# Splitting weights into halves beside attention: loads two parts ahead, stores half a step later, spread over 1.3 batches instead of 0.97

## The chip, the cores and the metric

The kernel runs on one core of one Trainium2 chip. The core has a matrix engine (TensorE, PE in the profile; its weight loads are PEld), VectorE (DVE), ScalarE (ACT), GpSimd (POOL), and SyncE (SP), which here issues every DMA. The engines run side by side, each through its own instructions in a fixed order, and wait for each other and for DMAs by semaphores. The metric is the device time of one execution in microseconds (us).

## The reference, cut to what matters

Eight sequences of 64 rows by 512 pass through six sublayers, each added to its input: cross attention with 32 heads on 8 key/value heads over a context of 1601 rows, a state space layer, a ternary feed forward layer, a second cross attention without weights, causal self attention, and an octonion feed forward layer. The change touches only the preparation of some weights, among them the output projection `Wo` of the first sublayer:

```python
q = (query @ Wq + bq).reshape(B, L, NKV, G, HDIM)
k_, v_ = jnp.split(kv @ Wkv + bkv, 2, axis=-1)
...
attn = jax.nn.softmax(scores, axis=-1)
o = jnp.einsum('bkglm,bmkd->blkgd', attn, v).reshape(B, L, NHEAD * HDIM)
return o @ Wo + bo
```

## The kernel before

**Halves.** Most products are computed in a format that carries fewer bits than float32. To keep the precision, an operand is split into a rounded part (high) and the rest (low), and a product is the sum of high x high, high x low and low x high, three matmuls. `split` (L100) does it with two instructions: ACT rounds a copy (L105, or L65 where the order is pinned), and DVE or POOL subtracts (L106). Weights that are used again and again are split once and stored in DRAM as pairs of halves.

**The main line.** `x_all` (L517) walks through 8 batches of 8 key/value heads, 64 units of about 41 us. A unit consists of six steps. In them stand the keys of the unit (`x_k`, L354: 12 matmuls of k_ps for each of four blocks of the context; the first block of the next unit is made in the last step), the values (`x_v`, v_ps, L334), the scores (`x_s`, s_ps, L385), and, for the unit before, the maximum (`x_max` L403, `x_spread` L412), the exponentials (`x_exp`: DVE adds at L426, ACT exponentials at L427, POOL sums at L429, L446, L448 and L452), their product with the values (`x_av`, o_ps, L464) and the end (`x_o`). In step 3 the key weights wk of the next unit are loaded (`x_w`, L346), in step 4 its queries q (L351). There is one buffer for wk, so its load can start when the last k_ps of the unit that reads it is done, and the next unit's first k_ps needs it some 8 us later. During batch 0 the queries of the next unit are computed as well (`q_head`, L252) and stored (d_q, L283); that unit's q is loaded from there.

After each unit of an odd batch `x_wo` (L492) applies the output projection to that unit's heads of two batches: four tiles of `Wo` halves are loaded (L508, wo<-d_wo, 512 KB each) and used in three matmuls each (w_ps, L511). `x_wo(1, 0)`, the first, adds the input and the bias bo before (L500, L501). It runs during unit (1, 2).

**Beside it.** Generators are advanced between the main line's pieces: `advance` (L1314) compares the cost that the main line has yielded, in units of a batch (`X_COST` = 236), with a generator's start, end and total cost, and runs its next pieces. `halves` (L606) is one of them: from 0.1 to 0.97 batches it loads, splits and stores 56 parts of 128 x 512: 32 of `Wo`, 8 of `W_outT`, 16 of `attnT` (queues L614, L617; d_wo, d_wout, d_wat). `prep` (L620) runs from the first unit of batch 1 to 2.0 batches and prepares the feed forward weights. After two batches the other five sublayers of those two follow as generators, too; the last pair's forms the tail, after the main line.

**Buffers.** The parts of `halves`, bo and the tiles of `x_wo` share one tag, "wo", with `WOB` = 3 buffers. A tile that finds no free buffer waits until an earlier one is released: a part, when its store has landed; a tile of `x_wo`, when its matmuls are done.

**The order of the work.** The program is recorded in Python order, and a scheduler then orders each engine's instructions by its own estimate of when they can start, with the program's order as priority. `Side` (L68) pins a generator's instructions on DVE, ACT and POOL to the program's order; DMAs on SP are not pinned. On the chip each engine goes through the resulting order, and an instruction that waits holds all behind it.

Of the kernel before, what the change touches and what calls it, by code (L numbers as in the profile page):

```python
# [8 lines left out]
FP = mybir.dt.float32  # L9
FR = mybir.dt.float32r  # L10
# [6 lines left out]
P = 128  # L17
D = 512
# [19 lines left out]
WOB = 3  # L38
# [40 lines left out]
class Kernel:  # L79
# [526 lines left out]
    def halves(self):  # L606

        nc, i = self.nc, self.i
        todo = [(i["Wo"][k * G + g], self.wo_s[k][:, g]) for k in range(NKV) for g in range(G)]
        todo += [(i["W_outT"][h], self.wout_s[h]) for h in range(NCH)]  # L610
        todo += [(i["attnT"][m, c], self.wat_s[m][c]) for m in range(4) for c in range(NC)]
        for src, dst in todo:
            t = self.sb("wo", [P, 2, D], FR, pool=self.xp, bufs=WOB)
            nc.sync.dma_start(out=t[:, 1].bitcast(FP), in_=src)  # L614
            yield 0.5
            self.split(t[:, 0], t[:, 1], t[:, 1].bitcast(FP), eng=nc.gpsimd)
            nc.sync.dma_start(out=dst, in_=t.bitcast(FP))  # L617
            yield 0.5

    def prep(self):  # L620
# [664 lines left out]
    def run(self):  # L1285
# [22 lines left out]
        def start(gen, now, cost, end):  # L1308
            env = {k: getattr(self, k) for k in ENV}
            if not self.tail:  # L1310
                env["nc"] = Side(self, PINNED)
            side.append({"gen": gen, "cost": cost, "got": 0.0, "t0": now, "end": end, "env": env})
# [18 lines left out]
        gi, now, xdone = 0, 0.0, 0.0  # L1331
        start(self.halves(), HALVES_START, HALVES_COST, HALVES_END)
        for cost, fin in self.x_all(list(range(B))):
# [33 lines left out]
SPAN = [3.1,3.1,2.6,0.2]  # L1367
PREP_END = 2.0
HALVES_START = 0.1
HALVES_END = 0.97  # L1370
HALVES_COST = 56.0
MAMBA_TAGS = ("a2", "lv", "bc", "xpad", "sm")
FFN_TAIL = (("l", 0), ("l", 1), ("a", 0), ("l", 2), ("a", 1), ("d", 0), ("a", 2), ("d", 1), ("d", 2))
# [116 lines left out]
```

## Time and profile before

| | |
|---|---|
| three runs | 2689.3 us median (2683.2 to 2691.5) |
| profiled execution | 2687.2 us, its span 2685.1 us |
| mean granted clock of PE | 0.983 |
| PE busy | 2549.7 us, 95% of the span |
| ACT, POOL busy | 1350.2 us (50%), 1247.6 us (46%) |
| casts of halves (ACT, L65, tile wo) | 56 of 0.62 us, from 86.3 to 379.4 us |
| subtractions of halves (POOL, L65, tile wo) | 56 of 1.29 us |
| `x_wo`'s matmuls (L511) | 384, from 420.2 to 2384.4 us |
| ACT's waits for loads of parts, 86 to 382 us | 26.8 + 11.2 + 5.8 us |
| DMA, median from issue to landing | wo<-d_wo 5.3 us, d_wo<-wo 5.7, d_wat<-wo 4.7, wo<-in_attnT 4.4; wk from 90 to 380 us 4.6 |

A line of waits reads: the engine and its line, what released it, the microseconds in total, how often, and the longest. A line of the timeline reads: start, duration, engine and line, operation, output<-input, count, and in brackets the idle time before and what ended it; SPq is SP's queue of DMA issues, and an issue's duration is that of the issue, not of the transfer. A line of windows reads: from:to, length, busy time (instructions), granted clock (1.00 is full speed), mean busy share of the 16 DMA engines, GB/s.

### The profile page before, as it was taken

To read this page: it belongs to the slowest core of one execution; us is meant where nothing else is said; L and a number is where in the kernel's file an instruction comes from. 1 tells how busy PE (TensorE), PEld (TensorE's weight loads), DVE (VectorE), ACT (ScalarE), POOL (GpSimd) and SP (SyncE) were. 2 spreads that over 40 slices of the span, in tenths; PEclk is the share of its full clock that TensorE was granted. 3 is DMA by queue.
4 is the path that set the end of the run, shared out by engine and by line. 5 is a ranking of instruction groups with operands and counts; after the bars stand their busy time and mean duration, and the time that the engine had idled before them with its cause. 6 is when DMAs were issued, how large, how long until landed. Compare 5 with 4: busy or idle time off the path is not lost.

```text
span 2685.1 us, 43976 instructions
## 1 busy us (share of the span) xinstructions
PE 2549.7 (95%) x16320; PEld 2269.3 (85%) x16320; DVE 1667.6 (62%) x2739; ACT 1350.2 (50%) x3128; POOL 1247.6 (46%) x1243
## 2 busy tenths in 40 slices
PE   7999999999999999999999999999999999977797
PEld 6988999999999899978989988988898898964544
DVE  4534357665687775545567676554657777668754
ACT  4545454344556554544555554544546545436433
POOL 2434463463368663521367457521239556405420
PEclk9999999999999999999999999999999999987899
DMA  9788876675213244764324452665343455466674
GB/s 308 225 295 276 281 239 190 203 240 180 67 66 105 68 133 150 232 190 145 97 98 148 149 161 89 216 201 164 102 135 92 137 159 155 143 226 216 234 261 166
DMA packets 311126, 466.08 MB, mean 174 GB/s; under 512 B 88440, under 2 KB 187768, under 8 KB 306432
## 3 DMA queue, kind: packets, MB, share of 16 engines
q1 hardware_dynamic: 310912, 463.28, 53.4%
q8 instruction: 128, 2.10, 0.3%
q14 instruction: 86, 0.70, 0.1%
HBM read 389.66 MB, written 73.53 MB: 173 GB/s over the span
## 4 chain that ended last, share of the span: by engine, by line
PE 68%; DMA 9%; DVE 9%; POOL 7%; issue 4%; ACT 3%; SPq 0%; POOLq 0%; DVEq 0%; ACTq 0%
PE v_ps L334 16%; PE k_ps L363 16%; PE o_ps L464 10%; PE s_ps L385 8%; POOL a L65 3%; PE w_ps L511 2%; PE acc L274 2%; DVE a L65 2%; PE acc L1077 2%; PE acc L801 2%; PE acc L1021 1%; PE acc L759 1%; PE acc L756 1%; POOL ss L452 1%; DMA b<-in_ctxT_dram 1%
## 5 line engine op out<-in xcount | busy, mean ns | idle before, releaser
L363 PE MATMUL k_ps<-cxb,wk 128*128 128x384 f32 x2304 | 470.3, 347 | 35.3 <-DVE mx L392 13.2
L334 PE MATMUL v_ps<-wv,cxb 128*128 128x256 f32 x3456 | 467.9, 281 | 1.0 <-DVE kt L109 0.6
L334 PEld LDWEIGHTS v_ps<-wv,cxb 128*128 128x128 f32 x3456 | 438.0, 188 | 19.3 <-issue 11.7
L363 PEld LDWEIGHTS k_ps<-cxb,wk 128*128 128x128 f32 x2304 | 405.3, 191 | 53.2 <-DVE mx L392 15.6
L464 PE MATMUL o_ps<-S,v 128*128 128x256 f32 (+1 forms) x1664 | 413.6, 381 | 7.4 <-DVE rw L479 4.0
L385 PE MATMUL s_ps<-q,kt 128*128 128x256 f32 (+1 forms) x2496 | 413.7, 299 | 5.2 <-DVE mx L392 2.4
L385 PEld LDWEIGHTS s_ps<-q,kt 128*128 128x128 f32 (+1 forms) x2496 | 342.8, 185 | 28.5 <-issue 6.9
L388 ACT COPY S<-s_ps 128x512 f32<-128x512 f32 (+1 forms) x448 | 241.9, 553 | 241.0 <-PE s_ps L385 236.6
L452 POOL TENSOR_TENSOR ss<-ss,S 128x512 f32<-128x512 f32 x254 | 349.3, 1375 | 14.7 <-ACT S L427 1.3
L392 DVE TENSOR_TENSOR mx<-s_ps,mx 128x512 f32<-128x512 f32 x256 | 175.1, 684 | 264.0 <-ACT S L388 262.7
L464 PEld LDWEIGHTS o_ps<-S,v 128*128 128x128 f32 (+1 forms) x1664 | 298.6, 190 | 46.7 <-issue 5.2
L429 POOL TENSOR_TENSOR ss<-S,S 128x512 f32<-128x512 f32 x64 | 84.5, 1320 | 469.4 <-ACT S L427 469.1
L108 ACT ACTIVATE kt<-k_ps,c_bk 128x384 fp32r<-128x384 f32 (+1 forms) x256 | 152.0, 594 | 246.9 <-PE k_ps L363 245.9
L426 DVE TENSOR_TENSOR S<-S,m_ps 128x512 f32<-128x512 f32 (+1 forms) x448 | 257.3, 640 | 20.5 <-PE m_ps L412 20.2
L427 ACT ACTIVATE S<-S 128x512 f32<-128x512 f32 (+1 forms) x448 | 246.7, 599 | 43.4 <-DVE S L426 42.7
L109 DVE SCALAR_TENSOR_TENSOR kt<-k_ps,c_bk,kt 128x384 fp32r<-128x384 f32 (+1 forms) x256 | 160.9, 629 | 158.0 <-ACT kt L108 156.5
L337 ACT COPY v<-v_ps 128x256 f32<-128x256 f32 (+1 forms) x416 | 152.5, 368 | 198.4 <-PE v_ps L334 196.0
L334 PE MATMUL v_ps<-wv,cxt 128*128 128x256 f32 (+1 forms) x1536 | 206.5, 282 | 1.5 <-DVE mx L392 1.0
L334 PEld LDWEIGHTS v_ps<-wv,cxt 128*128 128x128 f32 (+1 forms) x1536 | 192.7, 175 | 10.5 <-issue 3.4
L65 DVE TENSOR_TENSOR_SCAN a<-a,a 128x512 f32<-128x512 f32 x96 | 154.7, 1613 | 62.9 <-POOL a L65 62.8
L363 PE MATMUL k_ps<-cxt,wk 128*128 128x450 f32 x768 | 178.6, 375 | 1.4 <-DVE mx L392 1.3
L65 POOL TENSOR_TENSOR a<-a,bc 128x512 f32<-128x512 f32 x96 | 128.1, 1335 | 90.7 <-DVE a L65 90.7
(357 smaller groups left out, 3947.8 us busy)
## 6 DMA issues: line engine op xcount, KB each, us to landing
wo<-d_wo SPq DMA_DIRECT2D x128, 512.0 KB, 5.3
wk<-d_wk SPq DMA_DIRECT2D x63, 512.0 KB, 3.5
wv<-d_wv SPq DMA_DIRECT2D x31, 1024.0 KB, 5.7
cst<-in_ctxT_dram SPq DMA_DIRECT2D x96, 192.0 KB, 3.0
b<-in_ctxN_dram SPq DMA_DIRECT2D x36, 512.0 KB, 3.7
d_q<-q_t SPq DMA_DIRECT2D x32, 512.0 KB, 5.9
q<-d_q SPq DMA_DIRECT2D x64, 256.0 KB, 3.1
d_wo<-wo SPq DMA_DIRECT2D x32, 512.0 KB, 5.7
```

Of the source, the lines that this page charges most:

```text
L65: return lambda *a, **k: self.tc.keep_in_program_order(f(*a, **k))
L109: eng.scalar_tensor_tensor(lo, src, bias, hi.bitcast(FP), ALU.add, ALU.subtract)
L334: nc.tensor.matmul(ps[:r], lhsT=cx[:, a, c, o : o + r], rhs=w[:, m, c, :], start=k == 0, stop=k == 11)
L337: nc.scalar.copy(vt[:r], ps[:r])
L363: nc.tensor.matmul(ps[:, :wd], lhsT=w[:, a, c, :], rhs=cx[:, m, c, :], start=k == 0, stop=k == 11)
L385: nc.tensor.matmul(sp[:r, gi, :], lhsT=kt[:, a, o : o + r], rhs=q[:, m, :], start=k == 0, stop=k == 2)
L388: nc.scalar.copy(s[:r, :n], sp[:r, :n])
L392: nc.vector.tensor_tensor(mx, sp, S[0] if len(S) == 1 else mx, ALU.max)
L426: nc.vector.tensor_tensor(sv, sv, ps[:r, 1:2].to_broadcast([r, w, 256]), ALU.add)
L427: nc.scalar.activation(sv, sv, AF.Exp, scale=ISC)
L452: nc.gpsimd.tensor_tensor(ss, ss, S[n], ALU.add)
L464: nc.tensor.matmul(ps[:, 0], lhsT=self.v[(b, j, t)][:r, hc : hc + P], rhs=S[t // 2][:r, t % 2], start=t == 0, stop=t == NT - 1)
```

## The change

`halves` keeps its parts, their order and the instructions for each. Before, a step was: take a buffer and load; half a step later split and store. Now two loads are issued at the start; a step is: split; half a step later store, and load the part after the next one. The total cost is the same, and the end goes from 0.97 to 1.3 batches. `WOB` remains 3.

```diff
-        for src, dst in todo:
-            t = self.sb("wo", [P, 2, D], FR, pool=self.xp, bufs=WOB)
-            nc.sync.dma_start(out=t[:, 1].bitcast(FP), in_=src)
+        ts = {}
+
+        def load(k):
+            if k < len(todo):
+                ts[k] = self.sb("wo", [P, 2, D], FR, pool=self.xp, bufs=WOB)
+                nc.sync.dma_start(out=ts[k][:, 1].bitcast(FP), in_=todo[k][0])
+
+        load(0)
+        load(1)
+        yield 1
+        for k, (src, dst) in enumerate(todo):
+            t = ts.pop(k)
+            self.split(t[:, 0], t[:, 1], t[:, 1].bitcast(FP), eng=nc.gpsimd)
             yield 0.5
-            self.split(t[:, 0], t[:, 1], t[:, 1].bitcast(FP), eng=nc.gpsimd)
             nc.sync.dma_start(out=dst, in_=t.bitcast(FP))
+            load(k + 2)
             yield 0.5
...
-HALVES_END = 0.97
+HALVES_END = 1.3
```

## The prediction

> **What bounds the kernel now.** I read the page's first three parts, then the waits of TensorE (PE) and of SP's queue, then time windows.
>
> ```profile
> span 2685.1 us, 43976 instructions
> PE 2549.7 (95%) x16320; PEld 2269.3 (85%) x16320; DVE 1667.6 (62%) x2739; ACT 1350.2 (50%) x3128; POOL 1247.6 (46%) x1243
> ```
>
> PE is busy 95% of the span, so whatever delays PE counts in full, and waits of ScalarE (ACT) and GpSimd (POOL) count only where PE ends up waiting for them. PE's waits from 20 to 335 us, where the halves run:
>
> ```profile
> PE k_ps L363 <- DMA wk<-d_wk: 9.2, 5, 4.1
> PE acc L274 <- DVE q_t L109: 1.3, 1, 1.3
> ```
>
> Five times PE stands before the next head's keys, until the tile wk has landed. SP's own waits from 90 to 380 us say what held wk's load back:
>
> ```profile
> SPq L614 <- DMA d_wo<-wo: 68.4, 27, 6.5
> SPq L617 <- POOL wo L65: 32.0, 25, 3.7
> SPq L614 <- DMA d_wat<-wo: 20.0, 9, 5.8
> SPq L614 <- DMA d_wout<-wo: 18.6, 8, 4.7
> SPq L351 <- DMA d_q<-q_t: 10.5, 6, 3.2
> ```
>
> SP issues in order. 139 us of these 290 it stands before loads of halves (L614, 107 us, until an earlier store has left one of the three `wo` buffers) or before their stores (L617, 32 us, until POOL is done); wk's load stands behind. The worst case, SP and then PE:
>
> ```profile
> 180.25 1.72 SPq L247 DMA_DIRECT2D q_w<-in_Wq_dram  x1
> 182.06 1.28 SPq L617 DMA_DIRECT2D d_wo<-wo  x1
> 185.23 0.33 SPq L351 DMA_DIRECT2D q<-d_q  x1
> 185.61 0.46 SPq L346 DMA_DIRECT2D wk<-d_wk  x1
> ...
> 191.35 3.84 PE L363 MATMUL k_ps<-cxb,wk 128*128 128x384 f32 x12 [4.09 <-DMA wk<-d_wk]
> ```
>
> The buffer of wk was free at 179.59 (end of the last matmul that reads it); its load is issued 6.0 us late. PE by windows (time, busy, granted clock):
>
> ```profile
> 170.00:210.00 40.00, 35.91 (x213) 0.96 0.82 265
> 210.00:250.00 40.00, 38.01 (x235) 1.00 0.87 294
> 330.00:380.00 50.00, 47.18 (x314) 1.00 0.83 278
> 380.00:420.00 40.00, 40.00 (x276) 1.00 0.57 190
> 420.00:460.00 40.00, 40.00 (x274) 1.00 0.52 154
> ```
>
> From 90 to 380 us PE idles 12.0 us (9.2 for wk, 2.8 around the batch's end, 335 to 370 us), and one clock dip costs 40 x 0.04 = 1.6 us. So **13.6 us is all that the change can win** there. From 380 us, when the halves are done, PE idles nothing.
>
> **The change, part by part.** No arithmetic and no byte is added: 56 loads, 56 casts (622 ns), 56 subtractions (1292 ns), 56 stores, as before.
>
> *Loads two ahead.* SP is not pinned to program order, and the loads already go as soon as a buffer is free:
>
> ```profile
> 6.62 1.97 SPq L614 DMA_DIRECT2D wo<-in_Wo_dram  x3
> ```
>
> Three are issued by 8.6 us, the first cast runs at 86.3. The built program keeps the pattern: each load follows the store that frees its buffer. This edit alone I cost at nothing. *Stores half a step later*: the scheduler again places them by readiness, directly ahead of q and wk in five heads of seven, as before: nothing. [...]
>
> *Spread to 1.3 batches.* Before, 56 parts take 86 to 379 us, 5.2 us each, for 0.87 batches. Over 1.20 batches that is 404 us, 7.2 each, to about 490. If a part holds SP as long as now, SP is held 139/404 = 34% of the time and not 48%: x 0.72. The lateness of the six wk loads that count (from the end of the last matmul on the old wk to the issue at L346) is 0.8, 4.0, 6.0, 6.9, 3.5, 3.3 us, 24.5 in all. Of it 10.5 is q's load waiting for d_q to land, which the change does not touch; the other 14.0 shrinks to 10.1. So lateness falls by 16%, 3.8 us over the last five, which are the ones that PE waited for; each falls by less than PE's wait, so all 3.8 of the 9.2 us are saved. Of the 2.8 at the batch's end I take 1.2, of the clock's 1.6 half: **gain 5.8 us**, between 0 and 13.6.
>
> *What the longer spread runs into.* From `x_wo(1, 0)` on (PE 420 us), the output projection takes the same three `wo` buffers. Before, the halves had left them:
>
> ```profile
> 381.45 0.33 SPq L617 DMA_DIRECT2D d_wat<-wo  x1
> 381.83 1.26 SPq L508 DMA_DIRECT2D wo<-d_wo  x2
> ```
>
> The weights of `x_wo` were called 38 us ahead, and PE never waited long for them. After, some ten parts are still to come. The order in which the built program stands on SP, with what each waits for:
>
> ```
> store part A (POOL); store part B (POOL)
> load bo      (A's store landed: its buffer)
> load w0      (B's store landed)
> load w1      (POOL's add of bo)
> load part C  (PE has used w0)
> load w2      (PE has used w1)
> store part D (POOL); load wk
> load w3      (D's store landed)
> ```
>
> On PE, after the spread of the maximum (L412), stand 13 o_ps matmuls in a row, each waiting for an exponential, then w_ps with w0, and v_ps, s_ps and k_ps behind; before, that work stood between them. In the clock of the old trace: part B is cast after the copy of v at 419.68 (0.37), so at 420.05 + 0.62; POOL 1.29 gives 422.0; a d_wat store lands in 4.7 (426.7), w0 in 5.3: 432.0. PE is through the spread at 420.6 (mc is ready at 420.12). The adds (L426, 0.64 us each) and exponentials (L427) let the 13th o_ps go at 426, with 13 x 0.216 = 2.8 us of work in it. PE idles 432.0 - 420.6 - 2.8 = **8.6 us**. With the shortest landing seen for these tiles (2.6) and for w (4.3) it is 5.5; with the longest (8.0 and 7.4) 14.0.
>
> Three smaller ones. w3, behind D's store: 0.9 us. Casts of two parts whose loads wait until PE has used w3 stand on ACT before the next head's kt: 0.2 + 4.4 (load) + 0.62 + 0.59 + 0.63 = 6.4 us against 5.25 us of matmuls ahead (0.7 + 2.1 + 1.4 + 1.05): 1.2. The head after that repeats the pattern with fewer o_ps (nine) and one part ahead of w0: about 2.9, estimated at a third of the first. Together 5.0, between 0 and 7. The stall of six us before w0 is longer than the 4.09 us gap that was followed by the clock of 0.96, so I add its 1.6. **Loss 8.6 + 5.0 + 1.6 = 15.2 us**, between 5.5 and 22.6. [...]
>
> *Elsewhere.* The built program's order on PE is the old one again from the last heads of batch 1 to the tail; in the tail the scheduler orders anew. Nothing removed or added; PE idles 68 of the last 385 us, so a new order can win or lose: 0, with 5 us to both sides.
>
> **Sum.** 15.2 - 5.8 = +9.4 us on the profiled execution's 2687.2 (span 2685.1 and 2.1 around it), that is 2696.6. The median of the three runs is another 2.1 us higher, 2689.3; on it the sum gives 2698.7. I forecast **2698**.
>
> **Rivals.** *The gain comes whole, the projection's weights are in time* (faster). If wk is never late, 13.6 us come back; if the w loads reach the queue before the parts do, since the real stores land in 2.6 us or POOL is ahead, what is left of the loss is about 3. 2689.3 - 13.6 + 3 = 2679. It decides where w0 lands before PE's 13th o_ps, 6 us sooner than I reckon. For it: SP's 139 us are large, PE's gaps are all here. Against: w0 needs two landings in sequence after B's cast. *A wash.* The same waits, spread wider: gain 5, loss at its low end 5.5: 2690. For it: after 420 us SP and POOL are less loaded (DMA share 0.52 against 0.85), so landings are short. *Worse.* All three heads that overlap stall like the first, or the tail's new order costs 5 more: 2690 + 20 to 25, 2712. *The change does nothing, since the scheduler hoists loads anyway*: true of the loads, but the order on SP and PE did change; it goes with the wash.
>
> **Numbers.** Forecast case (2692 to 2705) 0.50; faster rival 0.17; wash 0.18; worse 0.15. About 0.3% (8 us) is what a measurement of this kernel can tell from no change: 2681 to 2697.4 is "same". The forecast case is split by this edge, 0.30 above and 0.20 below; so slower 0.45, same 0.40 (0.20 + 0.18 + 0.02 of the faster rival), faster 0.15. Range 2680 to 2712: from the faster rival to the worse one.
>
> **What would show it.** Right: PE idle from 90 to 380 us falls from 12.0 to some 7; the waits of ACT for wo's loads nearly go, and nothing comes of it; around 425 to 435 us a PE gap of about 6 us before w_ps, released by the load of wo from d_wo, and gaps among o_ps released by ACT; SP waits in L508. Wrong: no PE gap over 2 us before w_ps from 400 to 480 us (then the loss fails, and the time falls below 2690), wk waits that do not shrink, or a difference that arises after 2384 us.

## The result, and the profile after

The changed kernel takes 2701.9 us (median of 7 runs, 2694.4 to 2709.3), the kernel before 2687.9 (7 runs on the same chip, 2683.2 to 2691.5): a ratio of 1.0052, 95% interval 1.0040 to 1.0063. It is slower by half a per cent; the forecast was 2698. The profiled execution is the fastest of its seven, 2694.4 us (before: 2687.2), so the trace holds +7.2 us of a difference of +14; where the rest lies in the other runs no trace shows.

The page's first lines again, the profile after:

```profile
span 2692.3 us, 43979 instructions
PE 2554.8 (95%) x16320; PEld 2273.3 (84%) x16320; DVE 1666.3 (62%) x2739; ACT 1352.6 (50%) x3128; POOL 1251.9 (46%) x1243
```

The shares are the old ones; the page's top doesn't show the change at all. PE's waits from 20 to 335 us do:

```profile
PE k_ps L363 <- DMA wk<-d_wk: 0.4, 1, 0.4
```

The waits for wk, 9.2 us before, have all but gone. Windows of PE (time, busy, granted clock) show what came instead:

```profile
170.00:210.00 40.00, 40.00 (x248) 1.00 0.79 257
330.00:380.00 50.00, 49.73 (x344) 1.00 0.74 259
380.00:420.00 40.00, 35.08 (x211) 0.96 0.80 258
420.00:460.00 40.00, 35.58 (x215) 0.87 0.56 182
460.00:500.00 40.00, 35.59 (x224) 0.96 0.78 257
```

Where the halves alone ran, PE is now full. Where it used to be full, from 380 us on, it idles 13.7 of 120 us and the granted clock falls too. PE's timeline there:

```profile
409.87 7.57 PE L464 MATMUL o_ps<-S,v 128*128 128x256 f32 x26 [2.36 <-ACT S L427]
421.12 1.62 PE L511 MATMUL w_ps<-wo,ot 128*128 128x512 f32 x3 [3.68 <-DMA wo<-d_wo]
422.54 5.00 PE L334 MATMUL v_ps<-wv,cxb 128*128 128x256 f32 x23
...
434.81 2.88 PE L334 MATMUL v_ps<-wv,cxb 128*128 128x256 f32 x24
439.55 0.96 PE L511 MATMUL w_ps<-wo,ot 128*128 128x512 f32 x3 [1.86 <-DMA wo<-d_wo]
```

and SP's (in the changed kernel the stores of parts are L626, their loads L617):

```profile
409.01 1.50 SPq L626 DMA_DIRECT2D d_wat<-wo  x2
414.76 0.33 SPq L500 DMA_DIRECT2D wo<-in_bo_dram  x1
...
415.93 0.33 SPq L508 DMA_DIRECT2D wo<-d_wo  x1
418.74 0.33 SPq L508 DMA_DIRECT2D wo<-d_wo  x1
```

This is the predicted queue: two stores of parts, then bo's load, for which SP waits 4.2 us until the first store has landed because it takes that part's buffer, w0 behind the second store's landing, w1 behind POOL's add of bo. PE stands 3.68 us for w0. The v_ps behind it shows the second cost: 23 matmuls take 5.00 us, and 24 of the same kind 12 us later take 2.88; most of the first ones run at half speed (granted clock 0.50 from 422 to 426 us).

To add it up I compared the ends of each unit's last k_ps in both traces. The changed kernel is 13.5 us ahead at 388 us, 0.3 behind at 432, 11.3 behind at 744, 11.7 behind at the last unit, and 7.2 at the end. So it gains 13.5 us, loses 24.8, and ends 4.5 us less behind than it entered the tail. How exact that is, two runs below show: E5 and E6 turned out to be the program of before, and their traces differ from its trace by 1.2 and 1.8 us at the tenth unit, 4.9 and 0.2 at the last and 5.1 and -5.3 at the end. So the gain and the loss are clear of this spread, and the 4.5 us of the tail are not (E6's tail differs by 5.5).

**Theories.** *Main*: gain and loss both come from the spread, the gain since SP is held less often ahead of wk, the loss since the last parts share three `wo` buffers with `x_wo`. *Rival 1*: the loss comes from the parts' running beside `x_wo` and the preparation at all (queue, ACT, POOL, DMA). *Rival 2*: the gain comes from the new order of the loop, not from the spread.

### The profile page after: what moved, and what is told of

Its sections match the earlier page's. It is cut to its first block, busy times and chain, and to the rows that moved or that the text cites. A ratio compares the mean times of both kernels' runs of the same rounds, so it can differ in the third digit from the quotient of the medians.

```text
span 2692.3 us, 43979 instructions
## 1 busy us (share of the span) xinstructions
PE 2554.8 (95%) x16320; PEld 2273.3 (84%) x16320; DVE 1666.3 (62%) x2739; ACT 1352.6 (50%) x3128; POOL 1251.9 (46%) x1243
## 4 chain that ended last, share of the span: by engine, by line
PE 68%; DVE 9%; DMA 8%; POOL 8%; issue 4%; ACT 3%; SPq 0%; POOLq 0%; DVEq 0%; ACTq 0%
PE v_ps L334 16%; PE k_ps L363 15%; PE o_ps L464 9%; PE s_ps L385 8%; POOL a L65 3%; PE acc L274 2%; PE w_ps L511 2%; DVE a L65 2%; PE acc L811 2%; POOL ss L452 2%; PE acc L1087 2%; PE acc L1031 2%; PE acc L769 1%; PE acc L766 1%; DVE b L65 1%
## 5 line engine op out<-in xcount | busy, mean ns | idle before, releaser
L334 PEld LDWEIGHTS v_ps<-wv,cxb 128*128 128x128 f32 x3456 | 439.9, 189 | 19.5 <-issue 11.7
L464 PE MATMUL o_ps<-S,v 128*128 128x256 f32 (+1 forms) x1664 | 416.7, 383 | 12.3 <-ACT S L427 8.5
L427 ACT ACTIVATE S<-S 128x512 f32<-128x512 f32 (+1 forms) x448 | 247.1, 599 | 44.4 <-DVE S L426 43.8
```

The source lines that it names most:

```text
L334: nc.tensor.matmul(ps[:r], lhsT=cx[:, a, c, o : o + r], rhs=w[:, m, c, :], start=k == 0, stop=k == 11)
L427: nc.scalar.activation(sv, sv, AF.Exp, scale=ISC)
L464: nc.tensor.matmul(ps[:, 0], lhsT=self.v[(b, j, t)][:r, hc : hc + P], rhs=S[t // 2][:r, t % 2], start=t == 0, stop=t == NT - 1)
```

## The experiments

All ratios are to the kernel before, run on the same chip in the same rounds (its medians: 2685.4 to 2690.8 us). "Late" is the sum of the lateness of the first six wk loads behind their release, as in the prediction; "held" is SP's time before loads and stores of parts from 90 to 380 us.

| kernel | us, ratio (95%) | late | held | PE idle 90-380 | PE idle 380-520 |
|---|---|---|---|---|---|
| before | 2687.9 | 24.4 | 143 | 12.0 | 0.1 |
| after | 2701.9, 1.0052 (1.0040-1.0063) | 8.8 | 134 | 2.2 | 13.7 |
| E1 spread 1.3 alone | 2699.1, 1.0037 (1.0024-1.0051) | 13.6 | 149 | 3.6 | 9.6 |
| E2 new loop alone | 2675.2, 0.9966 (0.9949-0.9983) | 12.5 | 131 | 3.0 | 0.0 |
| E3 own buffers late | 2682.4, 0.9986 (0.9973-0.9999) | 9.8 | 130 | 5.0 | 3.7 |
| E4 end at 1.1 | 2683.2, 0.9991 (0.9979-1.0002) | 15.0 | 138 | 4.2 | 3.9 |
| E5 loads ahead alone | 2689.3, 1.0011 (0.9999-1.0023) | 24.9 | 139 | 11.2 | 0.1 |
| E6 late store alone | 2685.7, 1.0007 (0.9994-1.0020) | 26.1 | 134 | 12.7 | 0.0 |
| E7 new loop, end 1.03 | 2676.5, 0.9964 (0.9952-0.9976) | 12.8 | 137 | 3.0 | 0.0 |
| E8 new loop, end 0.85 | 2684.8, 1.0001 (0.9992-1.0010) | 16.3 | 113 | 9.9 | 0.0 |
| E9 half a step of shift | 2673.3, 0.9954 (0.9937-0.9972) | 13.2 | 133 | 5.3 | 0.3 |
| E10 quarter of a step | 2686.0, 0.9991 (0.9979-1.0003) | 20.3 | 134 | 9.8 | 0.0 |
| E11 parts on POOL's queue | 2748.1, 1.0220 (1.0189-1.0252) | 12.4 | 0 | 8.6 | 56.3 |
| E12 three quarters | 2685.7, 0.9981 (0.9968-0.9993) | 21.1 | 127 | 11.0 | 0.0 |

### E1: the spread alone

The old loop, with

```diff
-HALVES_END = 0.97
+HALVES_END = 1.3
```

> The old loop (load, then split and store half a step apart) with the end of the spread at 1.3 batches: the spread alone. Main theory (the spread gives both the gain of the first batch and the loss behind it): TensorE's idle time of 90 to 380 us falls from 12.0 us to 2 to 5 us, and 380 to 520 us holds 8 to 14 us of idle time with granted clocks under 0.97 in two or three of its windows, as with both parts; time 2694 to 2706 us. Rival (the order of the loop makes the gain): 90 to 380 us keeps 9 us or more, the loss stays, time 2708 to 2716 us.

The gain is there without the new loop: at the tenth unit, some 390 us, it stands at 10.8 us. So is the loss, but smaller: from -10.8 to +2.8 us at 733, that is 13.6 us and not 24.8. PE waited 6.8 us for wo and ran at 0.96 and 0.91 in two windows. The spread makes both, as the main theory says. But the trace ends 12.3 us behind, and 6.7 of that come in the tail, which takes 343.0 us. The eleven traces whose tail has the order of before take 330.8 to 337.7 us there; E1 and the changed kernel have other orders there, with 343.0 and 331.7. What the spread costs in the tail stays open.

### E2: the new loop alone

The changed loop, with the end back:

```diff
-HALVES_END = 1.3
+HALVES_END = 0.97
```

> The new loop (loads two ahead, store half a step behind the split) with the end of the spread at 0.97 batches as before: the order of the loop alone. Main theory: nothing of the gain and nothing of the loss, so idle time of 9 to 13 us from 90 to 380 us, under 2 us from 380 to 520 us, and 2683 to 2693 us. Rival (the order of the loop makes the gain, the spread the loss): 2 to 5 us of idle time from 90 to 380 us, time 2672 to 2680 us.

A miss for the main theory and a hit for rival 2: the new loop has the gain by itself (11.7 us ahead at the tenth unit, 13.2 at the end of the main line) and none of the loss. PE's waits from 90 to 380 us, and a window that was 35.58 at 0.87 after:

```profile
PE k_ps L363 <- DMA wk<-d_wk: 0.7, 2, 0.4
```

```profile
420.00:460.00 40.00, 40.00 (x272) 1.00 0.60 183
```

So each part of the change alone takes most of the wk waits away (2.2 of 9.2 us are left in E1, 0.7 here), and the spread adds little to that but its cost. The reason for E2 was the opposite of what I had costed, and E5 to E10 and E12 look for it.

### E3: the last parts in other buffers

The changed kernel; the 12 parts that are loaded behind the end of batch 0 take a tag with two buffers of the later preparation:

```diff
-                ts[k] = self.sb("wo", [P, 2, D], FR, pool=self.xp, bufs=WOB)
+                late = self.cpl
+                ts[k] = self.sb("b4" if late else "wo", [P, 2, D], FR, pool=late or self.xp, bufs=2 if late else WOB)
```

> The changed kernel, but the parts that are loaded behind the end of batch 0 (12 of them) take buffers of the tag b4, which only the first pieces of the later preparation use, so that x_wo of batch 1 has its three buffers for itself. Main theory (the loss comes from the shared buffers): the waits of w_ps for wo from 400 to 520 us go (under 1 us), the idle time from 380 to 520 us falls from 13.8 us to under 4 us, the granted clock there is 0.98 or more, and the time 2672 to 2684 us. Rival (the loss comes from the parts' running beside x_wo and the preparation at all, through SyncE's queue, ACT, POOL and the DMA): 8 us or more stay idle there and the time is 2693 us or more.

The time falls from 2701.9 to 2682.4 us with the same loop, spread and number of parts, and the first w_ps runs at 411.47 us instead of 421.12. Windows, and PE's wait for the weights from 380 to 520 us (1.4 us, where under 1 was expected):

```profile
380.00:420.00 40.00, 38.50 (x258) 1.00 0.81 265
420.00:460.00 40.00, 39.42 (x253) 1.00 0.77 261
```

```profile
PE w_ps L511 <- DMA wo<-d_wo: 1.4, 2, 1.2
```

The DMA share in these windows is no lower than after (0.81 and 0.77 against 0.80 and 0.56), and the loss has shrunk to 5.4 us (9.3 ahead at some 390 us, 3.9 at 730). So some four fifths of it is the shared buffers; running beside `x_wo` at all (rival 1) is worth at most the rest, 5.4 us.

### E4: the end ahead of the overlap

The changed loop, with the end of the spread at 1.1 instead of 1.3 batches.

> The changed kernel with the end of the spread at 1.1 batches, which is ahead of the first x_wo of batch 1 (it begins at some 1.17 batches). Main theory: most of the gain (2 to 6 us idle from 90 to 380 us instead of 12.0) and little of the loss (under 5 us idle from 380 to 520 us), time 2674 to 2684 us. Rival (what costs time is that the parts run beside batch 1 and the preparation at all): something between, 2688 to 2698 us, with idle time of 5 us or more from 380 to 520 us that no buffer of wo releases.

The waits of w_ps for wo are 0.6 us: without the overlap there is no such loss. But a wk came late at 217 us (6.9) and one at 393 us (5.3), each with a PE gap of over 3 us, so that the gain is smaller than in E2. The same loop with another end has other late heads, which was the first hint of what follows.

### E5 and E6: each half of the new loop alone

E5, with the end at 0.97: loads two ahead, the store right behind its split.

```diff
         load(1)
-        yield 1
         for k, (src, dst) in enumerate(todo):
             t = ts.pop(k)
-            self.split(t[:, 0], t[:, 1], t[:, 1].bitcast(FP), eng=nc.gpsimd)
             yield 0.5
+            self.split(t[:, 0], t[:, 1], t[:, 1].bitcast(FP), eng=nc.gpsimd)
             nc.sync.dma_start(out=dst, in_=t.bitcast(FP))
```

> End of the spread at 0.97 batches as before; the loads are two parts ahead, but the store stands right behind its split. Theory L (the loads made ahead take the hold off SyncE's queue ahead of wk): idle time of 3 to 5 us from 90 to 380 us, time 2673 to 2681 us, as with the whole new order. Theory S (the later store does it): 8 to 12 us of idle time, 2683 to 2691 us. Theory P (neither: any change moves each load by a few places against the store of its buffer, and the lateness of wk goes up and down with the place): something between, and the lateness of wk differs head by head from that of the new order.

E6, with the end at 0.97: the old loop, the store half a step later.

```diff
             yield 0.5
             self.split(t[:, 0], t[:, 1], t[:, 1].bitcast(FP), eng=nc.gpsimd)
+            yield 0.5
             nc.sync.dma_start(out=dst, in_=t.bitcast(FP))
-            yield 0.5
```

> End of the spread at 0.97 batches; each load stands in its own step as before, and only the store stands half a step behind its split. Theory L: nothing of the gain, idle time of 8 to 12 us from 90 to 380 us, 2683 to 2691 us. Theory S: 3 to 5 us of idle time, 2673 to 2681 us. Theory P: something between, with other heads late than before.

Neither does anything. More than that: in both built programs the order of the instructions is that of the kernel before on all five engines, instruction for instruction. The scheduler puts loads and stores where their buffers and data allow, wherever the loop names them. Theories L and S are out, and these two runs show what the same program measures as: 1.0011 and 1.0007.

What is left of E2 is the `yield 1` ahead of its loop, without which the first split would come at half a step: every cast, and with it every store and load, is half a step later. (With it the new loop's yields add up to 57 and not 56, so what stayed the same is the constant of the total cost alone.)

### E7 and E8: the new loop with other ends

The changed loop with the end at 1.03 and at 0.85 batches.

> The whole new order with the end of the spread at 1.03 batches, still ahead of x_wo of batch 1. Theories L and S: the gain of the new order stays, 2 to 5 us of idle time from 90 to 380 us, none of the loss (under 2 us from 380 to 520 us), 2671 to 2680 us. Theory P: idle time of 3 to 9 us from 90 to 380 us, 2674 to 2688 us.

> The whole new order with the end of the spread at 0.85 batches: the parts denser by 0.87 / 0.75 = 1.16. If the order removes the hold whatever the density: 3 to 5 us of idle time from 90 to 380 us, 2673 to 2681 us. If the density counts beside it (the share of the spread in the gain): 6 to 10 us of idle time, 2679 to 2688 us. Theory P: the same range, but with heads late that are not those that are late at 0.97.

1.03 is as good as 0.97. At 0.85 the gain is gone, and other heads are late (6.5 us at 179 us, where E2 has 1.5; 1.1 at 224, where E2 has 4.8) although SP was held for 113 us only. That speaks against SP's total hold as the measure, and for where the parts fall (theory P).

### E9, E10 and E12: the old loop, shifted

One line in the kernel before, nothing else; half a step in E9, 0.25 in E10, 0.75 in E12:

```diff
+        yield 0.5
         for src, dst in todo:
             t = self.sb("wo", [P, 2, D], FR, pool=self.xp, bufs=WOB)
```

> The kernel before with one line more: the generator of the parts gives back half a step ahead of its first load, so that all casts, loads and stores of the parts come half a step (some 3 us) later; the end of the spread stays at 0.97 batches, the loop is the old one. Theory P (the loads ahead and the later store change no instruction's place; what the new loop does is the yield ahead of it, which shifts all parts by half a step, and the gain comes from where the parts then fall): idle time of 2 to 5 us from 90 to 380 us, time 2672 to 2681 us, as with the whole new order. Rival (the two edits of the loop together do it, though neither does alone): 8 to 12 us of idle time, 2683 to 2691 us.

> The kernel before with a quarter of a step (some 1.5 us) ahead of the first load of the parts. If a later phase is better in itself (less beside something that comes before), about half the gain: 5 to 8 us of idle time from 90 to 380 us, 2678 to 2685 us. If the gain is the chance of each place against each wk: anything from 1 to 13 us of idle time and 2671 to 2692 us, with other heads late than at no shift and at half a step.

> The kernel before with three quarters of a step (some 4.5 us) ahead of the first load of the parts. So far the idle time of TensorE from 90 to 380 us was 12.0 us without a shift, 9.8 us with a quarter and 3.0 and 5.3 us with half a step. If a later phase is better in itself: 5 us of idle time or less, 2671 to 2678 us. If the gain is the chance of where the parts fall against each wk: more than at half a step is as likely as not, 6 to 12 us of idle time and 2679 to 2690 us, with lateness moved to other heads.

E9 has E2's built order on PE, DVE, ACT and POOL, and all but two places of it on SP, and it has its time; its idle time, 5.3 us, is just above the range. The gain of the new loop is this half step, some 2.6 us of 5.2 per part. It isn't "later is better": idle time from 90 to 380 us is 12.0, 9.8, 5.3 (3.0 in E2), 11.0 us at shifts of 0, 1/4, 1/2 and 3/4, and the ratios are 1, 0.9991, 0.9954 and 0.9981. What the shift moves is seen at the unit (or head) ahead of which PE waited longest. SP's queue in the kernel before, ahead of the lines that the prediction shows:

```profile
169.57 1.30 SPq L617 DMA_DIRECT2D d_wo<-wo  x1
177.49 0.33 SPq L614 DMA_DIRECT2D wo<-in_Wo_dram  x1
```

and in E2 (store L626, load L617):

```profile
168.37 0.32 SPq L626 DMA_DIRECT2D d_wo<-wo  x1
...
175.34 0.33 SPq L617 DMA_DIRECT2D wo<-in_Wo_dram  x1
175.80 0.59 SPq L247 DMA_DIRECT2D q_w<-in_Wq_dram  x1
176.96 0.33 SPq L626 DMA_DIRECT2D d_wo<-wo  x1
179.00 0.32 SPq L351 DMA_DIRECT2D q<-d_q  x1
179.37 0.45 SPq L346 DMA_DIRECT2D wk<-d_wk  x1
```

It is the same, nineteenth part. Before, its load stands directly behind the store that frees its buffer; SP waits 6.6 us for the landing, 2 us before wk's release at 179.59, and then has a backlog to issue. In E2 that store was issued at 168.37 with three other DMAs between, SP waits 1.5 us, and wk's load goes 1.5 us behind its release and not 6.0. That is one head. At other late heads SP's last wait ahead of wk is for another thing, mostly q's load waiting for d_q (E12 at 178 us: 2.4 us of it, wk 5.1 us late); that the place of the parts decides there too is argued from the runs' idle times, not shown line by line.

### E11: the parts' DMAs on POOL's queue

```diff
-            nc.sync.dma_start(out=t[:, 1].bitcast(FP), in_=src)
+            nc.gpsimd.dma_start(out=t[:, 1].bitcast(FP), in_=src)
...
-            nc.sync.dma_start(out=dst, in_=t.bitcast(FP))
+            nc.gpsimd.dma_start(out=dst, in_=t.bitcast(FP))
```

> The kernel before, but POOL issues the loads and stores of the parts instead of SyncE; loop, phase and end of the spread (0.97) as before. Theory (the wk waits come from SyncE's being held by the parts' DMAs): the holds of SyncE at the two lines go, wk is issued within 2 us of its release at every head but those that wait for d_q, and TensorE's idle time for wk from 90 to 380 us falls from 9.2 us to under 2 us. The time depends on what the holds do on POOL: if its other work (the splits, cxb) has room, 2672 to 2680 us; if POOL's holds delay cxb or the row sums, TensorE waits for these instead and the time is 2685 to 2720 us. Rival (wk is late for another reason, the load on the DMA engines): 6 us or more of waits for wk stay.

The lateness halves with SP no longer held, and PE's waits for wk fall from 9.2 to 3.5 us: SP's holds made most of them, but not under 2 us, since SP's other waits (q's load for d_q alone 16.3 us from 90 to 380 us) remain. The time lies beyond both ranges, since it goes wrong at the place where the changed kernel does. POOL waited 105 us for casts from 90 to 380 us and the parts ran on to 479 us and beyond; bo's and w0's loads stood behind them. PE's wait and SP's wait from 380 to 520 us:

```profile
PE w_ps L511 <- DMA wo<-d_wo: 43.1, 2, 42.8
```

```profile
SPq L500 <- DMA d_wat<-wo: 48.6, 2, 27.8
```

One PE gap of 42.85 us is 43 of the 60 us that it costs: a larger dose of the shared buffers.

## Why the prediction was right, and where it was off

**The sum.** 2698 was forecast and 2701.9 measured; on the profiled execution 2696.6 and 2694.4. Both of its halves exist, at the places named, but both terms are some half of what was measured: gain 5.8 forecast, 13.5 measured; loss 15.2 forecast, 24.8 measured in that trace (the range had 5.5 to 22.6). The two errors, 7.7 and 9.6 us, nearly cancel, and that the sum fits so well is luck. The tail was forecast at 0 with 5 us to both sides and measured -4.5, which is no more than two traces of one program differ by.

**"Loads two ahead ... nothing", "stores half a step later ... nothing".** Right for what they name (E5, E6: not one instruction moves). ACT's waits for loads of parts fell from 43.8 to 11.5 us after, but the spread alone (E1) takes them to 5.0, and the loads ahead alone (E5) leave them at 45.4. What I did not cost is the `yield 1` in the same edit: it shifts all parts by half a step, and that alone makes 0.9954 (E9).

**The gain.** The step that failed is "if a part holds SP as long as now ... x 0.72", lateness in proportion to the hold. SP was held 143 us before (139 in the lines shown, the rest in smaller ones) and 134 after (E1: even 149), 6% less and not 28; the six wk loads are late by 24.4 and 8.8 us (E1: 13.6). At the head shown above it was the place: a load close behind the store of its own buffer shortly before wk is released. And lateness turns into PE's waits only beyond a slack, 1.9 to 4.9 us per head before (6.02 us late gave 4.09, 6.85 gave 1.99, 3.49 gave 0.70); so about half of the lateness (12.4 to 13.6 us in E1, E2, E7, E9 and E11) left 0.7 to 3.5 of the 9.2 us. In E1 the spread does it, in E9 the shift; that the spread does it in general, and not by falling well, isn't shown: ends of 0.85, 1.03 and 1.1 with the same loop give 9.9, 3.0 and 4.2 us of idle time without a trend.

**The overlap.** Right in mechanism: E3 takes the sharing away and four fifths of the loss go; E4 avoids the overlap and w_ps hardly waits (0.6 us). PE idles 13.7 us from 380 to 520 us after, and 3.7 in E3. The queue on SP came in the order told. Sizes: the first stall, 8.6 us forecast, is 2.36 + 3.68 = 6.0 (26 o_ps went in the row, not 13). The "three smaller" ones, 5.0 in all, are w3 1.86 (0.9 forecast), kt nothing (1.2) and the next head 1.44 + 2.95 + 1.45 = 5.8 (2.9): 7.7. (For the 2.95 the profile names no releaser; the gap stands before w_ps, whose weights were called 3.7 us before its end, behind the landing of a part's store.) From 520 to 700 us another 1.8. With the clock's 8.4 below that is 23.9 of the 24.8.

**The clock** is the term that was missed most: 1.6 us forecast, (0.04 + 0.13 + 0.04) x 40 = 8.4 measured. I let one gap dip it; four did. Short windows after show it, behind the gap of 2.36 us:

```profile
410.00:412.00 2.00, 2.00 (x6) 0.55 0.91 270
412.00:414.00 2.00, 2.00 (x7) 0.60 1.05 425
414.00:416.00 2.00, 2.00 (x11) 1.00 0.43 147
```

The gaps of 3.68, 1.86 and 2.95 us were followed by clocks of 0.50 as well, those of 1.44 and (before) 1.99 us by 1.00. Behind the gap of 1.86 us after, and behind that of 1.99 us before:

```profile
442.00:444.00 2.00, 2.00 (x7) 0.50 1.05 304
```

```profile
237.00:239.00 2.00, 2.00 (x12) 1.00 0.98 336
```

So the four gaps cost another 2.1 us of work each on average. The length of a gap alone doesn't tell whether it is followed by a lower clock: 1.86 us was, 1.99 us before was not, and neither was E4's gap of 3.2 us (its window from 380 to 420 us, 36.84 of 40 us busy, has a granted clock of 1.00). What decides beside the length isn't shown.

**Rivals.** *Faster* failed: w0 landed 3.7 us after PE's last o_ps. *The change does nothing* holds for two of its three edits and not for the shift beside them. *Worse*: two heads stalled, not three, and the profiled tail was no longer than before. The other six runs are 6 to 15 us longer than the profiled one, more than the spread of before; which stalls grew there stays open. Not run: the changed loop with a store right behind its split beside `x_wo`. E1's loss ahead of the tail is smaller than the changed kernel's (13.6 against 24.8 us); whether by the loop beside `x_wo` or by its half step isn't told apart.

**The best version** is E9, one line in the old loop: 2673.3 us, 0.9954 (0.9937 to 0.9972) of before, with E2 and E7 the same within their intervals. It is a lucky phase and would have to be found again after any edit. Having no load queued right behind the store of its own buffer should take that one hold away; this wasn't run, and it would not end the waits: in E11, with no part on SP at all, wk is still 12.4 us late in all and PE waits 3.5 us for it.

## What to carry to other kernels

Before costing an edit in a generator, compare the built order on each engine: two of three edits here moved nothing, and a start offset of half a step that looked like bookkeeping was worth 0.46%. A queue's total hold said little here (143 us before and 149 in E1, with 12.0 and 3.6 us of PE's idle time); look at what stands ahead of the few DMAs that the bound engine waits for, and at their slack. Work that is spread past a stage's end meets the next stage's use of the same buffers: count who holds them there, and reckon with a dip of the clock behind a gap of PE: it cost 2.1 us of work on average behind four gaps of 1.86 to 3.68 us here, and nothing behind those of 1.99 us before and 3.2 us in E4.

## What was not expected of the hardware

SP's issues were slower when they came in a row in a stretch where the DMA engines were busy: before, from 90 to 380 us (DMA share 0.85), the fourth and later issues of an unbroken row took 1.19 us at the median (36 issues), the first ones 0.33 (88). It isn't the kind of DMA: the stores d_wo<-wo alone took 0.33 as first (11) and 1.21 as fourth or later (11). From 520 to 700 us (share 0.60) the fourth and later took 0.4 (10 issues); these are other DMAs, and whether the share makes the difference isn't shown. At the head shown above a hold cost twice, the wait and a backlog behind it: the five issues behind the held load took 4.9 us.
